# One RWKV-6 block on one core: norm mixes from tiles that ScalarE scales in PSUM

## The chip, the cores and the metric

The kernel runs on one core of a Trainium2 chip. The metric is the device time of one execution in microseconds (us), as the median of several runs. The engines are named as in the profile: PE (TensorE), DVE (VectorE), ACT (ScalarE), POOL (GpSimd) and SP (SyncE, which here only issues DMAs). All arithmetic is in float32.

## The reference, cut to what matters

The input `x` holds 32 sequences of 128 tokens with 512 features. Each sequence goes through one RWKV-6 block. Both of its halves begin with a layer norm and a "token shift": the row before minus the row itself, where the row before the first token comes from a given state.

```python
def _ln(x, w, b): ...          # (x - mean) * rsqrt(var + EPS) * w + b
def _token_shift(xn, prev_row):
    first = (prev_row - xn[:, 0])[:, None]
    rest = xn[:, :-1] - xn[:, 1:]
    return jnp.concatenate([first, rest], axis=1)

xn = _ln(x, ln1_w, ln1_b)                       # first norm
sx = _token_shift(xn, state[:, i1])
xxx = jnp.tanh((xn + sx * maa_x) @ maa_w1)...   # then @ maa_w2, five parts
x5 = xn[:, :, None] + sx[:, :, None] * (maa_stack + xxx)
...                                             # w, r, k, v, g from x5; the recurrence; group norm
x = x + att * g @ Wo.T
xn2 = _ln(x, ln2_w, ln2_b)                      # second norm
sx2 = _token_shift(xn2, state[:, i0])
xk = xn2 + sx2 * ffn_maa_k
xr = xn2 + sx2 * ffn_maa_r
rr = jax.nn.sigmoid(xr @ ffn_Wr.T)
kk = jnp.square(jax.nn.relu(xk @ ffn_Wk.T))
x = x + rr * (kk @ ffn_Wv.T)
```

The row difference of the first norm, `sx`, is used six times (once for `maa_x`, five times for `x5`); that of the second norm, `sx2`, only in the two mixes `xk` and `xr`.

## The kernel before, in words

The 32 sequences are worked in eight groups of four. A group's tile of tokens is 512 columns wide (4 sequences x 128 tokens) and the 512 features lie in four chunks `e` of 128 partitions. For each group these streams exist, each a Python generator:

- `front_mix`: loads `x`, does the first norm, the row difference `sx`, the mix `xin`, and then the five mixed inputs `x5` (lines L433 on PE, L438 and L440 on DVE).
- `front_proj` and `front_gate`: the projections w, k, v, r and g (L389 on PE), evicted by ACT (L499) and sent by DMA into a layout with one head per partition.
- `prep`: the states and products that the recurrence needs (L562, L583, L593, L601 and others on DVE).
- the recurrence, for eight groups one after the other, in units: ACT fills a PSUM tile `sc` (L638) and a column (L649), POOL multiplies and adds (L663, L667), DVE scans (L685) and multiplies (L687, into `rm`), and PE sums over eight transposes (L720, into `acc`).
- `back`: the group norm, the output projection (L788 transposes, L797 scaling on ACT, L799 on DVE, L808 matmuls, L817 adding to `x`), the second norm, and the feed-forward part (the `fk` matmuls at L389, `fr` at L861, `fv` at L877). For the last group it runs twice, on two halves of two sequences each, with half-size tiles (`last1`, `last2`).

Both norms go through `layernorm_T`. It computes the statistics, normalises the rows on ACT (L342), transposes each chunk on PE into a PSUM tile `ps` (L358), and ACT evicts that tile, with the norm's weight and bias, into the SBUF tile `xnT` (L352). `xnT` has one column more than the tokens, for the row before the first token, so the row before and the row itself are the same tile read with an offset of 0 and 1. When all four chunks are there, one DVE instruction makes the row difference (L366; L370 for a half):

```python
nc.vector.tensor_tensor(
    sx.t.rearrange("p e (b t) -> p (e b) t", t=L), xnT[:, :, 0:L], xnT[:, :, 1 : L + 1], ALU.subtract)
```

Then `mix` makes each mix with four DVE instructions (L383), `sx * v + xnT`, all three tiles in SBUF: once after the first norm (`xin`), twice after the second (`xk` ahead of the `fk` matmuls, `xr` after the first of them has been issued).

The order of instructions on each engine is not written by hand. Every generator yields operations with their engine, an estimated duration, what they read and write and which buffer they need, and a list scheduler (`Plan`) takes, again and again, the operation that could start first by its own estimates. Among those that could start within `EPSILON` of the first it prefers the one whose stream is most due, by the table `DUE`. The result is one fixed order per engine; at run time an engine waits where its next instruction's inputs or buffer aren't there. `PE_GAP` is what the planner adds to every operation of PE. Buffers have tags: `ps` is a ring of four PSUM tiles that all matmul results, the transposes and some DVE products share; `sc` has two PSUM tiles, `acc` one; `mx` three SBUF tiles, `xnT` and `sx` one each.

Of the kernel before, what the change touches and what calls it, by code (L numbers as in the profile page):

```python
# [8 lines left out]
F32 = mybir.dt.float32  # L9
I32 = mybir.dt.int32  # L10
AF = mybir.ActivationFunctionType
ALU = mybir.AluOpType
# [23 lines left out]
PE, DVE, ACT, POOL, SP = range(5)  # L36
PASS = 0.43
GAP = 0.034
PE_GAP = 0.09

WINDOW, KEEP, WAKE = 3.41, 0.4, 0.7
LANDING = 2.0
HOP = (0.2, 0.05, 0.05, 0.04, 0.08)
EPSILON = 0.0988


DUE = {"rec": (-0.042, 0.99), "mix": (-1.355, -0.244), "proj": (-1.038, 0.138), "gate": (0.041, 0.061), "prep": (0.365, 1.041), "back": (0.971, 2.191), "last1": (0.877, 1.621), "last2": (1.287, 1.307)}


class Buf:  # L50
# [129 lines left out]
def rwkv6_block(ctx: ExitStack, tc: tile.TileContext, x, prev, s0, vecs, u, maa_w1, maa_w2,  # L180
# [40 lines left out]

    vec = const.tile([P, NV, NE], F32, name="vec")
    pv = const.tile([P, 2, NE, B], F32, name="pv")
    u_sb = const.tile([P, S], F32, name="u_sb")
    w1_sb = const.tile([P, NE, 5 * XM], F32, name="w1_sb")
    w2p = const.tile([P, 4, E], F32, name="w2p")
# [74 lines left out]
    def part(us, bs):  # L301

        return us if len(bs) == GB else us * len(bs) / GB + 0.03

    def layernorm_T(g, src, sums, vw, vb, which, need=None, bs=range(GB)):

        b0, nb_ = bs[0], len(bs)
        bsl, cols = slice(b0, b0 + nb_), slice(b0 * L, (b0 + nb_) * L)  # L310
        if sums is None:
            xh = src
            stats, mv = yield Op(DVE, 0.88, r=[(src, b0)], w=[(0, b0), (1, b0)], alloc=["stats", "mv"])
            for b in bs:
                if b != b0:
                    yield Op(DVE, 0.88, r=[(src, b)], w=[(stats, b), (mv, b)])
                nc.vector.bn_stats(stats[:, b, :], src[:, b, :])
                nc.vector.bn_aggr(mv[:, b, :], stats[:, b, :])
            stats.open = False
            mean, var, scale = mv[:, bsl, 0], mv[:, bsl, 1], 1.0  # L320
        else:
            mv = sums
            yield Op(DVE, 0.16, r=[(mv, b) for b in bs], w=[(mv, "m")])
            mean, var, scale = mv[:, bsl, 0], mv[:, bsl, 1], 1.0 / E
            nc.vector.tensor_scalar(mean, mean, -1.0 / E, None, ALU.mult)
            xh = None
            for b in bs:
                if xh is None:
                    (xh,) = yield Op(ACT, 0.83, r=[(src, b), (mv, "m")], w=[(0, b), (mv, ("v", b))], alloc=["ev"])
                else:  # L330
                    yield Op(ACT, 0.83, r=[(src, b), (mv, "m")], w=[(xh, b), (mv, ("v", b))])
# [12 lines left out]
        rstd.open = nb.open = False  # L344
        (xnT,) = yield Op(ACT, 0.25, w=[(0, "p")], alloc=["xnT"], need=need)
        nc.scalar.copy(xnT[:, :, 0].rearrange("p (e b) -> p e b", b=GB)[:, :, bsl],
                       pv[:, 1 - which, :, g * GB + b0 : g * GB + b0 + nb_])
        late = []

        def evict(e, pt):  # L350
            yield Op(ACT, part(0.78, bs), r=[(pt, None)], w=[(xnT, e)], end=[pt])
            nc.scalar.activation(xnT[:, e * GB + b0 : e * GB + b0 + nb_, 1 : L + 1], bt(pt[:, cols]), AF.Identity,  # L352
                                 bias=col(vb, e), scale=col(vw, e))

        for e in range(NE):
            (pt,) = yield Op(PE, 0.11 * nb_, r=[(xh, None)], w=[(0, None)], alloc=["ps"])
            for b in bs:
                nc.tensor.transpose(pt[:, b * L : (b + 1) * L], xh[:, b, e * P : (e + 1) * P], ident)  # L358
# [6 lines left out]
        if nb_ == GB:  # L365
            nc.vector.tensor_tensor(  # L366
                sx.t.rearrange("p e (b t) -> p (e b) t", t=L), xnT[:, :, 0:L], xnT[:, :, 1 : L + 1], ALU.subtract)
        else:
            xv = xnT.t.rearrange("p (e b) t -> p e b t", b=GB)[:, :, bsl]
            nc.vector.tensor_tensor(sx.t.rearrange("p e (b t) -> p e b t", t=L)[:, :, bsl], xv[:, :, :, 0:L],  # L370
                                    xv[:, :, :, 1 : L + 1], ALU.subtract)
        return xnT, sx

    def mix(xnT, sx, v, bs=range(GB)):

        o = None
        b0, b1 = bs[0], bs[-1] + 1
        for e in range(NE):
            if o is None:
                (o,) = yield Op(DVE, part(0.74, bs), r=[(xnT, None), (sx, None)], w=[(0, e)], alloc=["mx"], port=True)  # L380
            else:
                yield Op(DVE, part(0.74, bs), r=[(xnT, None), (sx, None)], w=[(o, e)], port=True)
            nc.vector.scalar_tensor_tensor(bt(o[:, e, b0 * L : b1 * L]), bt(sx[:, e, b0 * L : b1 * L]), col(v, e),  # L383
                                           xnT[:, e * GB + b0 : e * GB + b1, 1 : L + 1], ALU.mult, ALU.add)
        return o

    def matmuls(p, w, xin, e, cols=slice(0, N)):
        for c in range(NE):
# [12 lines left out]
    def front_mix(g, d):  # L401
# [2 lines left out]
        if g == 0:  # L404
            constants()
        need = (lambda: "ln2" in data[g - 3]) if g > 2 else None
        xnT, sx = yield from layernorm_T(g, xt, None, V_LN1W, V_LN1B, 0, need)
        xin = yield from mix(xnT, sx, V_MAAX)
# [334 lines left out]
    def back(g, d, bs=range(GB), W=None):  # L743
# [81 lines left out]
        xnT, sx = yield from layernorm_T(g, x1, sums, V_LN2W, V_LN2B, 1, need, bs)  # L825
        fkt = yield from get("fk", fk)
        xk = yield from mix(xnT, sx, V_FK, bs)
        frt = yield from get("fr", fr)
        kk, late = None, []
        for e in range(NE + 1):  # L830
            if e < NE:
                (p,) = yield Op(PE, 2 * len(bs) * PASS, r=[(xk, None), (fkt, None)], w=[(0, None)], alloc=["ps"])
                matmuls(p[:, cols], fkt, xk, e, cols)
                late.append(p)
                if e == 0:
                    xr = yield from mix(xnT, sx, V_FR, bs)
                    xnT.open = sx.open = False
# [100 lines left out]
```

## Time and profile before

| | us |
|---|---|
| median of three runs (lowest, highest) | 1603.89 (1602.61, 1604.11) |
| the profiled execution, its own time | 1601.06 |
| its span, first to last instruction | 1599.3 |
| L366 and L370, row differences | 49.1 and 2.4 |
| L383, mixes, 88 full and 16 half tiles | 101.3 |

In a line of engine sums, the first number is the busy time of the engine in us, then its share of the span, then its instructions. The slices cut the span into 40 parts of 40 us; each digit is the busy share in tenths, 9 for 90% or more. In a group's line stand the line of the code, engine, operation, output and inputs by name, their sizes, the count, the busy time in us and the mean of one in ns, and after the second bar the idle time of that engine just before these instructions with what ended it. In a line of waits stand who waited for whom, the sum in us, the number of waits and the longest. In the table by stage, each engine has its busy us in the stretch and its instructions.

### The profile page before, as it was taken

How to read it: one execution, taken by the hardware profiler on the slowest of the kernel's cores; microseconds unless marked ns; L12 is line 12 of the kernel's file. 1: busy time of each engine (PE TensorE's matmuls, PEld its weight loads, DVE VectorE, ACT ScalarE, POOL GpSimd, SP SyncE). 2: the span in 40 equal slices, each digit the busy share in tenths (PEclk: the TensorE clock that was granted, in tenths of full speed). 3: DMA queues.
4: the chain of work that ended last, by engine and by line, in shares of the span. 5: the costliest groups of instructions: out<-in, count | busy, mean ns of one | idle time of the engine just before them, and what ended most of it. 6: DMA issues, size and time to landing. Idle time of an engine off the chain costs nothing.

```text
span 1599.3 us, 16204 instructions
## 1 busy us (share of the span) xinstructions
PE 1477.0 (92%) x5216; PEld 768.9 (48%) x5216; DVE 1374.0 (86%) x1687; ACT 565.9 (35%) x1109; POOL 940.9 (59%) x545
## 2 busy tenths in 40 slices
PE   5997898999999999999999999999999999977978
PEld 2343454454554554545454555445444454444544
DVE  6448999999989999989989999899988899688752
ACT  3222332443334333353333433343323433234242
POOL 4026792886637775578455765478645784477700
PEclk9998999999999999999999999999999999988989
DMA  6220332323224231422323332242313222230230
GB/s 214 60 75 27 93 93 79 120 94 99 66 94 140 66 119 50 138 86 75 103 73 129 119 99 70 96 135 66 119 56 106 92 91 101 85 132 2 75 108 27
DMA packets 126790, 146.85 MB, mean 92 GB/s; under 512 B 8081, under 2 KB 76305, under 8 KB 125681
## 3 DMA queue, kind: packets, MB, share of 16 engines
q1 hardware_dynamic: 91888, 129.03, 24.6%
q10 hardware_dynamic: 34816, 16.79, 3.6%
q8 instruction: 41, 0.67, 0.2%
q14 instruction: 45, 0.36, 0.1%
HBM read 94.41 MB, written 17.83 MB: 70 GB/s over the span
## 4 chain that ended last, share of the span: by engine, by line
PE 50%; DVE 36%; issue 6%; POOL 3%; DMA 2%; ACT 2%; SPq 0%; DVEq 0%; ACTq 0%; POOLq 0%
PE ps L389 14%; DVE sc L685 9%; PE ps L877 7%; PE acc L720 7%; PE ps L808 7%; PE ps L861 7%; DVE rm L687 6%; DVE ps L438 4%; DVE mx L440 3%; DVE mx L383 3%; PE ps L433 2%; DVE sx L366 2%; POOL am L663 2%; PE ps L467 1%; POOL a L667 1%
## 5 line engine op out<-in xcount | busy, mean ns | idle before, releaser
L663 POOL TENSOR_TENSOR am<-v,k 128x1024 f32<-128x1024 f32 x256 | 630.7, 2464 | 185.5 <-DVE k L562 65.4
L389 PE MATMUL ps<-mx,wt 128*128 128x512 f32 (+1 forms) x1312 | 581.2, 590 | 20.3 <-DVE blk L522 6.6
L667 POOL TENSOR_TENSOR a<-am 128x504 f32<-128x504 f32 x256 | 279.6, 1092 | 359.6 <-DVE sc L685 314.8
L389 PEld LDWEIGHTS ps<-mx,wt 128*128 128x128 f32 x1312 | 244.4, 192 | 298.5 <-issue 260.2
L687 DVE TENSOR_TENSOR rm<-sc,r 128x1024 f32<-128x1024 f32 x256 | 312.9, 1222 | 43.7 <-PE acc L720 28.0
L720 PEld LDWEIGHTS acc<-by_head,rm 128*128 128x128 f32 x2176 | 250.1, 143 | 170.5 <-DVE rm L687 81.0
L720 PE MATMUL acc<-by_head,rm 128*128 128x128 f32 x2176 | 285.8, 279 | 48.7 <-DVE rm L687 42.6
L685 DVE TENSOR_TENSOR_SCAN sc<-sc,a 128x512 f32<-128x512 f32 x256 | 312.7, 1222 | 9.0 <-POOL a L667 4.9
L638 ACT COPY sc<-w 128x512 f32<-128x512 f32 x256 | 151.4, 592 | 269.6 <-DVE rm L687 206.1
L433 PE MATMUL ps<-tha,w2p 128*128 128x512 f32 x256 | 129.6, 618 | 8.6 <-DVE mx L440 5.7
L438 DVE SCALAR_TENSOR_TENSOR ps<-ps,vec,sx 128x512 f32<-128x512 f32 x160 | 119.8, 749 | 19.9 <-PE ps L433 19.9
L649 ACT COPY a<-st 128x8 f32<-128x8 f32 x256 | 51.8, 203 | 217.5 <-DVE sc L685 206.3
L808 PE MATMUL ps<-wt,mx 128*128 128x512 f32 x256 | 118.9, 611 | 2.4 <-DVE mx L799 1.0
L861 PE MATMUL ps<-wt,mx 128*128 128x512 f32 x256 | 115.2, 592 | 0.0
L440 DVE TENSOR_TENSOR mx<-ps,xnT 128x512 f32<-128x512 f32 x160 | 110.4, 690 | 4.8
L383 DVE SCALAR_TENSOR_TENSOR mx<-sx,vec,xnT 128x512 f32<-128x512 f32 (+1 forms) x104 | 101.3, 1032 | 0.5
L877 PE MATMUL ps<-wt,ev 128*128 128x512 f32 x224 | 100.8, 592 | 0.0
L499 ACT COPY blk<-ps 128x512 f32<-128x512 f32 x96 | 56.0, 583 | 80.3 <-PE ps L389 62.8
L808 PEld LDWEIGHTS ps<-wt,mx 128*128 128x128 f32 x256 | 47.8, 195 | 61.7 <-issue 50.7
L861 PEld LDWEIGHTS ps<-wt,mx 128*128 128x128 f32 x256 | 47.9, 190 | 56.9 <-issue 55.0
L433 PEld LDWEIGHTS ps<-tha,w2p 128*128 128x128 f32 x256 | 44.1, 195 | 49.4 <-issue 23.7
L366 DVE TENSOR_TENSOR sx<-xnT 128x2048 f32<-128x2048 f32 x15 | 49.1, 3272 | 17.8 <-ACT xnT L352 17.8
(97 smaller groups left out, 1173.8 us busy)
## 6 DMA issues: line engine op xcount, KB each, us to landing
x<-in_x SPq DMA_DIRECT2D x15, 1024.0 KB
wt<-in_wk SPq DMA_DIRECT2D x8, 1024.0 KB
wt<-in_wr SPq DMA_DIRECT2D x8, 1024.0 KB
wt<-in_wg SPq DMA_DIRECT2D x8, 1024.0 KB
dgate<-blk SPq DMA_DIRECT2D x32, 256.0 KB
wt<-in_wo SPq DMA_DIRECT2D x8, 1024.0 KB
wt<-in_fk SPq DMA_DIRECT2D x8, 1024.0 KB
wt<-in_fr SPq DMA_DIRECT2D x8, 1024.0 KB
```

The costliest lines, as they stand in the source:

```text
L389: nc.tensor.matmul(p, lhsT=w[:, c, e * P : (e + 1) * P], rhs=xin[:, c, cols], start=(c == 0), stop=(c == NE - 1))
L433: nc.tensor.matmul(pp.t, lhsT=w2[:, e * P : (e + 1) * P], rhs=lo, start=True, stop=True)
L438: nc.vector.scalar_tensor_tensor(pp.t, pp.t, col(V_MAA + m, f), sx[:, f, :], ALU.add, ALU.mult)
L440: nc.vector.tensor_tensor(bt(x5[:, f, :]), bt(pp.t), xnT[:, f * GB : (f + 1) * GB, 1 : L + 1], ALU.add)
L663: nc.gpsimd.tensor_tensor(am.t, v[:, ds, :], k[:, q : q + 1, :].to_broadcast([P, DH, L]), ALU.mult)
L667: nc.gpsimd.tensor_tensor(a[:, :, 1:T2], am2[:, :, 0 : T2 - 1, 0], am2[:, :, 0 : T2 - 1, 1], ALU.add)
L685: nc.vector.tensor_tensor_scan(scf, scf, a.t.rearrange("p d n -> p (d n)"), 0.0, ALU.mult, ALU.add)
L687: nc.vector.tensor_tensor(pair(rm.t), sc.t.unsqueeze(3).to_broadcast([P, DH, T2, 2]), r2[:, q : q + 1, :, :].to_broadcast([P, DH, T2, 2]), ...
L720: nc.tensor.matmul(acc[:, i, :], lhsT=rm[:, i, :], rhs=by_head, is_transpose=True, start=(q == 0 and i % 4 == 0), stop=(q == S), skip_grou ...
L808: nc.tensor.matmul(p.t, lhsT=att[:, c, b * L : (b + 1) * L], rhs=wot[:, c, :], start=(c == 0), stop=(c == NE - 1))
L861: nc.tensor.matmul(p.t, lhsT=xr[:, c, b * L : (b + 1) * L], rhs=frt[:, c, :], start=(c == 0), stop=(c == NE - 1))
L877: nc.tensor.matmul(p2.t, lhsT=kv[:, c, b * L : (b + 1) * L], rhs=fvt[:, c, :], start=(c == 0), stop=(c == NE - 1))
```

## The change

Four things are changed, and the planner's constants with them.

1. **First norm.** After ACT has evicted a transposed chunk into `xnT`, it scales the same chunk once more, in place in PSUM, with the same weight and bias. DVE then makes that chunk's row difference (row before from `xnT` in SBUF, row itself from PSUM) and at once its mix `xin`. The row difference is therefore four instructions in place of one.
2. **Second norm.** The row difference is not made. A mix is written as `before * m + (1 - m) * itself`. For `xk`, ACT scales the chunk in PSUM in place with the constants `(1 - m) * weight` and `(1 - m) * bias`, and one DVE instruction per chunk adds `m` times the row before. For `xr` (a new function `receptance`), ACT writes `(1 - m)` times the chunk of `xnT` into a new `ps` tile, and DVE adds in the same way.
3. **Constants.** Four small POOL instructions at the start make `ffn`, the products with `1 - m`.
4. **Order.** `back` may begin only when the group's gates are there too; `PE_GAP` goes from 0.09 to 0.04, `EPSILON` from 0.0988 to 0.02, and every entry of `DUE` has another value. The instructions of the other streams stay the same in kind and number, but their order on each engine differs in many places.

```diff
-PE_GAP = 0.09
+PE_GAP = 0.04
...
-EPSILON = 0.0988
+EPSILON = 0.02
...
-DUE = {"rec": (-0.042, 0.99), "mix": (-1.355, -0.244), "proj": (-1.038, 0.138), "gate": (0.041, 0.061), "prep": (0.365, 1.041), "back": (0.971, 2.191), "last1": (0.877, 1.621), "last2": (1.287, 1.307)}
+DUE = {"rec": (0.073, 0.928), "mix": (-1.183, -0.487), "proj": (-1.108, 0.725), "gate": (-0.487, 0.788), "prep": (11.173, 11.194), "back": (1.114, 2.212), "last1": (-8.358, -8.236), "last2": (1.752, 11.136)}
...
         nc.sync.dma_start(out=vec, in_=vecs)
+        nc.gpsimd.tensor_scalar(ffn[:, 0, :], vec[:, V_FK, :], -1.0, 1.0, ALU.mult, ALU.add)
+        nc.gpsimd.tensor_scalar(ffn[:, 2, :], vec[:, V_FR, :], -1.0, 1.0, ALU.mult, ALU.add)
+        nc.gpsimd.tensor_tensor(ffn[:, 1, :], ffn[:, 0, :], vec[:, V_LN2B, :], ALU.mult)
+        nc.gpsimd.tensor_tensor(ffn[:, 0, :], ffn[:, 0, :], vec[:, V_LN2W, :], ALU.mult)
...
         def evict(e, pt):
-            yield Op(ACT, part(0.78, bs), r=[(pt, None)], w=[(xnT, e)], end=[pt])
+            yield Op(ACT, part(0.78, bs), r=[(pt, None)], w=[(xnT, e)])
             nc.scalar.activation(xnT[:, e * GB + b0 : e * GB + b0 + nb_, 1 : L + 1], bt(pt[:, cols]), AF.Identity,
                                  bias=col(vb, e), scale=col(vw, e))
+            yield from use(xnT, e, pt, tiles)
...
-        (sx,) = yield Op(DVE, part(2.3, bs), r=[(xnT, None)], w=[(0, None)], alloc=["sx"], port=True)
...
-            nc.vector.scalar_tensor_tensor(bt(o[:, e, b0 * L : b1 * L]), bt(sx[:, e, b0 * L : b1 * L]), col(v, e),
-                                           xnT[:, e * GB + b0 : e * GB + b1, 1 : L + 1], ALU.mult, ALU.add)
...
+        def use(xnT, e, pt, tiles):
+
+            yield Op(ACT, 0.75, w=[(pt, None)])
+            nc.scalar.activation(pt.t, pt.t, AF.Identity, bias=col(V_LN1B, e), scale=col(V_LN1W, e))
+            sx, xin = tiles
+            yield Op(DVE, 0.69, r=[(xnT, e), (xnT, "p"), (pt, None)], w=[(sx, e)])
+            nc.vector.tensor_tensor(bt(sx[:, e, :]), row(xnT, e, 0), bt(pt.t), ALU.subtract)
+            yield Op(DVE, 0.75, r=[(pt, None), (sx, e)], w=[(xin, e)], end=[pt])
+            nc.vector.scalar_tensor_tensor(xin[:, e, :], sx[:, e, :], col(V_MAAX, e), pt.t, ALU.mult, ALU.add)
...
-        yield Op(DVE, 0.0, need=lambda: d.get("rec"))
+        yield Op(DVE, 0.0, need=lambda: "rec" in d and ("gate", NE - 1) in d)
...
+        def use(xnT, e, pt, tiles):
+
+            yield Op(ACT, part(0.75, bs), w=[(pt, None)])
+            nc.scalar.activation(pt[:, cols], pt[:, cols], AF.Identity, bias=ffn[:, 1, e : e + 1], scale=ffn[:, 0, e : e + 1])
+            (xk,) = tiles
+            yield Op(DVE, part(0.75, bs), r=[(xnT, e), (xnT, "p"), (pt, None)], w=[(xk, e)], end=[pt])
+            nc.vector.scalar_tensor_tensor(bt(xk[:, e, cols]), row(xnT, e, 0, bs), col(V_FK, e), bt(pt[:, cols]),
+                                           ALU.mult, ALU.add)
+
+        def receptance(xnT):
+            xr = None
+            for e in range(NE):
+                if xr is None:
+                    pr, xr = yield Op(ACT, part(0.75, bs), r=[(xnT, e)], w=[(0, None)], alloc=["ps", "mx"])
+                else:
+                    (pr,) = yield Op(ACT, part(0.75, bs), r=[(xnT, e)], w=[(0, None)], alloc=["ps"])
+                nc.scalar.activation(bt(pr[:, cols]), row(xnT, e, 1, bs), AF.Copy, scale=ffn[:, 2, e : e + 1])
+                yield Op(DVE, part(0.75, bs), r=[(xnT, e), (pr, None)], w=[(xr, e)], end=[pr])
+                nc.vector.scalar_tensor_tensor(bt(xr[:, e, cols]), row(xnT, e, 0, bs), col(V_FR, e), bt(pr[:, cols]),
+                                               ALU.mult, ALU.add)
+            return xr
...
-            xr = yield from mix(xnT, sx, V_FR, bs)
+            xr = yield from receptance(xnT)
```

More of the change, by code (lines that the diff above doesn't have):

```diff
@@ L223, in rwkv6_block @@
     pv = const.tile([P, 2, NE, B], F32, name="pv")
+    ffn = const.tile([P, 3, NE], F32, name="ffn")
     u_sb = const.tile([P, S], F32, name="u_sb")
@@ L303, in part, with layernorm_T @@
         return us if len(bs) == GB else us * len(bs) / GB + 0.03
-    def layernorm_T(g, src, sums, vw, vb, which, need=None, bs=range(GB)):
+    def layernorm_T(g, src, sums, vw, vb, which, use, take, need=None, bs=range(GB)):
         b0, nb_ = bs[0], len(bs)
@@ L350, in evict @@
         def evict(e, pt):
-            yield Op(ACT, part(0.78, bs), r=[(pt, None)], w=[(xnT, e)], end=[pt])
+            yield Op(ACT, part(0.78, bs), r=[(pt, None)], w=[(xnT, e)])
             nc.scalar.activation(xnT[:, e * GB + b0 : e * GB + b0 + nb_, 1 : L + 1], bt(pt[:, cols]), AF.Identity,
                                  bias=col(vb, e), scale=col(vw, e))
+            yield from use(xnT, e, pt, tiles)
         for e in range(NE):
-            (pt,) = yield Op(PE, 0.11 * nb_, r=[(xh, None)], w=[(0, None)], alloc=["ps"])
+            if e == 0:
+                pt, *tiles = yield Op(PE, 0.11 * nb_, r=[(xh, None)], w=[(0, None)], alloc=["ps", *take])
+            else:
+                (pt,) = yield Op(PE, 0.11 * nb_, r=[(xh, None)], w=[(0, None)], alloc=["ps"])
             for b in bs:
@@ L363, in layernorm_T, with row @@
         yield from evict(*late.pop(0))
-        (sx,) = yield Op(DVE, part(2.3, bs), r=[(xnT, None)], w=[(0, None)], alloc=["sx"], port=True)
[L365 to L383, printed above, removed]
-                                           xnT[:, e * GB + b0 : e * GB + b1, 1 : L + 1], ALU.mult, ALU.add)
-        return o
+        return (xnT, *tiles)
+    def row(xnT, e, shift, bs=range(GB)):
+        return xnT[:, e * GB + bs[0] : e * GB + bs[-1] + 1, shift : shift + L]
     def matmuls(p, w, xin, e, cols=slice(0, N)):
@@ L406, in front_mix @@
         need = (lambda: "ln2" in data[g - 3]) if g > 2 else None
-        xnT, sx = yield from layernorm_T(g, xt, None, V_LN1W, V_LN1B, 0, need)
-        xin = yield from mix(xnT, sx, V_MAAX)
+        def use(xnT, e, pt, tiles):
[6 more added lines that the diff above has]
+            nc.vector.scalar_tensor_tensor(xin[:, e, :], sx[:, e, :], col(V_MAAX, e), pt.t, ALU.mult, ALU.add)
+        xnT, sx, xin = yield from layernorm_T(g, xt, None, V_LN1W, V_LN1B, 0, use, ("sx", "mx"), need)
         d["xin"] = True
@@ L824, in back @@
         need = (lambda: "mixed" in data[g + 2]) if g + 2 < NG else None
-        xnT, sx = yield from layernorm_T(g, x1, sums, V_LN2W, V_LN2B, 1, need, bs)
+        def use(xnT, e, pt, tiles):
[10 more added lines that the diff above has]
+                    pr, xr = yield Op(ACT, part(0.75, bs), r=[(xnT, e)], w=[(0, None)], alloc=["ps", "mx"])
+                else:
+                    (pr,) = yield Op(ACT, part(0.75, bs), r=[(xnT, e)], w=[(0, None)], alloc=["ps"])
[4 more added lines that the diff above has]
+            return xr
+        xnT, xk = yield from layernorm_T(g, x1, sums, V_LN2W, V_LN2B, 1, use, ("mx",), need, bs)
         fkt = yield from get("fk", fk)
-        xk = yield from mix(xnT, sx, V_FK, bs)
         frt = yield from get("fr", fr)
@@ L835, in back @@
                 if e == 0:
-                    xr = yield from mix(xnT, sx, V_FR, bs)
-                    xnT.open = sx.open = False
+                    xr = yield from receptance(xnT)
+                    xnT.open = False
                     d["ln2"] = True
```

## Prediction

> **What bounds the kernel now.** I read the busy line and the slices first, then the chain, the costliest groups, a table of busy time by stage, and who ended TensorE's waits.
>
> ```profile
> PE 1477.0 (92%) x5216; PEld 768.9 (48%) x5216; DVE 1374.0 (86%) x1687; ACT 565.9 (35%) x1109; POOL 940.9 (59%) x545
> PE   5997898999999999999999999999999999977978
> DVE  6448999999989999989989999899988899688752
> PE 50%; DVE 36%; issue 6%; POOL 3%; DMA 2%; ACT 2%; SPq 0%; DVEq 0%; ACTq 0%; POOLq 0%
> ```
>
> PE and DVE are both full in the middle, and the chain that ended last changes between them; ScalarE (ACT) has room. The share averages over stages, so I asked for busy time by stage (columns: PE, PEld, DVE, ACT, POOL, each with its instructions; then clock and DMA):
>
> ```profile
> 150.00:200.00 50.00, 42.81 (x151) 21.75 (x151) 48.58 (x53) 16.16 (x33) 36.93 (x22) 0.89 0.24 74
> 200.00:400.00 200.00, 185.17 (x686) 96.99 (x684) 192.12 (x237) 72.39 (x146) 139.99 (x79) 0.98 0.31 97
> ...
> 800.00:1000.00 200.00, 195.93 (x708) 102.01 (x707) 186.91 (x222) 75.64 (x147) 128.79 (x71) 1.00 0.30 98
> ```
>
> From 150 to 400 us DVE bounds: 240.7 of 250 us busy, PE 228.0. From 400 to 1400 us PE bounds: the five stretches sum to 970.5 of 1000 us, DVE to 920.4. So a cheaper DVE can win there only what PE still loses to DVE. Who ended PE's waits between 400 and 1200 us:
>
> ```profile
> PE acc L720 <- DVE rm L687: 9.9, 12, 1.9
> PE ps L389 <- ACT ev L851: 3.1, 4, 1.0
> PE ps L433 <- DVE mx L440: 2.9, 4, 1.7
> PE ps L358 <- ACT xnT L352: 1.7, 4, 0.4
> ```
>
> With the small rows DVE ended 15.8 us of PE's waits there, and 5.5 us more in 1200 to 1400: 21.3 us out of 29.5 us of PE idle time.
>
> The rows that the change deletes, and those that price what it adds:
>
> ```profile
> L366 DVE TENSOR_TENSOR sx<-xnT 128x2048 f32<-128x2048 f32 x15 | 49.1, 3272 | 17.8 <-ACT xnT L352 17.8
> L383 DVE SCALAR_TENSOR_TENSOR mx<-sx,vec,xnT 128x512 f32<-128x512 f32 x88 | 94.8, 1133 | 0.5
> L440 DVE TENSOR_TENSOR mx<-ps,xnT 128x512 f32<-128x512 f32 x160 | 110.4, 690 | 4.8
> L438 DVE SCALAR_TENSOR_TENSOR ps<-ps,vec,sx 128x512 f32<-128x512 f32 x160 | 119.8, 749 | 19.9 <-PE ps L433 19.9
> L797 ACT ACTIVATE ps<-ps,vec 128x512 f32<-128x512 f32 x28 | 20.9, 751 | 10.1 <-PE ps L788 9.9
> L472 ACT ACTIVATE blk<-ps,vec 128x512 f32<-128x512 f32 x32 | 21.9, 685 | 27.9 <-DMA w<-blk 16.8 <-PE ps L467 8.8 <-PE acc L720 2.3
> ```
>
> The reader is to see that a mix from two SBUF tiles (L383) takes 1133 ns where the same operation with one operand in PSUM (L438) takes 749.
>
> [...] at 770.86 us, while POOL stood idle (768.7 to 776.3), four L383 took 2.74 us (685 ns each); at 20.59 us, beside POOL's L292, four took 4.30 us (1075 ns each). [...]
>
> **The change part by part.**
>
> DVE removed: L366 49.1, its half form L370 2.4, L383 101.3 (94.8 and 6.5 for halves): 152.8 us. DVE added: first norm, eight groups of four subtractions at 0.690 (L440's form) and four mixes at 0.750 (L438's): 46.1. Second norm: 28 full and 8 half tiles, each mixed twice: 56 x 0.750 + 16 x 0.482 [...] = 49.7. Sum 95.8; DVE does 57 us less. Per steady group: the first norm 3.3 + 4 x 1.08 = 7.6 becomes 5.8, the second 3.3 + 8 x 1.08 = 11.9 becomes 6.0, so -7.7 us. Bounds of the unseen mixes: 0.69 (L868, no pointer scalar) to 0.80; 4 us in all either way.
>
> ACT added: scaling in place, 60 x 0.751 and 8 x 0.532 (L797's two forms), 49.3; the receptance copies from SBUF to PSUM with one pointer, 28 x 0.685 and 8 x 0.47, 23.0: 72 us. ACT goes from 566 to 638 us, 40% of the span. It lies beside other work, but ACT's queue also carries the recurrence's fills (L638, L649), which now stand behind evictions that wait for a transpose. They had slack: ACT waited 206 us for L687 to give an sc tile back. POOL gets four 128x4 instructions at the start; its 7.2 us of idle time before L337 hides them. The DMAs stay as many (484 from SP, 256 from ACT), and POOL's other instructions too.
>
> By stage, against the profiled execution's own 1601.1 us (span 1599.3; the median of the runs is 2.8 us above it):
>
> - **0 to 150 us: 0.** The first mix would feed PE (L412) about 4 us sooner, but DVE then still has eight statistics to do (L317, L318) from x tiles that land at 25.9 us, and the order after keeps them ahead of the first L438. That wait for DMA is late next and hides the gain.
> - **150 to 400: -5.7.** DVE bounds. The first norm at 241 us (2.27 + 4.42) becomes 5.8, the second's row difference and first mix at 391 (3.11 + 4.71) becomes 3.0.
> - **400 to 1400: -14.** DVE loses 42 us of 920, but PE can only give back the 21.3 us it waited for DVE. The row difference and its mixes stand as blocks of 7 to 9 us in DVE's queue, with recurrence units behind them; in the order after they are single instructions between units. I take two thirds; the last third stays because L687 in turn waits for PE to free its rm tile (21.9 us in this stage). Next late is PE itself.
> - **1400 to 1530: -3.** The norm at 1450 us (2.29 + 7.35) becomes 6.0; recurrence units there also run into POOL (78 of 100 us busy).
> - **1530 to the end: +2.** The order after puts the second half's first two transposes ahead of the first half's last four. They wait for the y that DVE finished at 1536.5, where PE before had begun at 1530.2. Seven ACT scalings (about 0.49 us apart) then end near 1540 and the first matmuls of L808's kind with them; before, that block ended at 1541.3 at a lowered clock. Between 0 and +5.
> - **PSUM tiles: +5.** The ps ring has four buffers. The order shows 36 more ps tiles (636 to 672), and 68 norm tiles held through one more ACT and one or two DVE instructions: 104 tiles, over 2 us longer each. What PE pays for it no row shows. Below: 0, since the tiles of the first mix and L440 already pass with 5.7 + 4.4 us of PE waits; above: 0.4 us a tile (the longest wait of L358 for a norm tile), 42 us. I take 0.05.
>
> Sum -15.7: 1585.4 against 1601.1, so 1588 as a median of runs. The re-tuned planner constants have no row; I take 0 with 10 us either way, since the order keeps the same 854 PE rows and the same sequence of stages.
>
> **The rivals.** 0.2% of 1604 is 3.2 us, about what a measurement of this kernel can tell from no change.
>
> - **DVE and PE give back more** (0.20). In the chain L383 and L366 hold 4.8% of the span, 77 of the 153 us that go. If the chain shortens in that proportion, 57 x 77/153 = 29 us go, and the smaller blocks win a few more: 1570 to 1575. Against it: behind these links PE had only 29.5 us idle in 1000.
> - **PE bounds it all** (0.14). The freed DVE time shows as idle time; only 150 to 400 us gains, less the ps tiles: 1598 to 1606. For it: PE's 97%.
> - **Slower: the ps ring** (0.20). PE and DVE queues run in a fixed order. A transpose, or a matmul of fk, waits for a ps buffer that is held for a scaling or a mix queued behind recurrence units, and all of PE's queue stands behind it. With 20.7 us of gain it decides from 0.20 us a tile on; at 0.4 it costs 42 and the kernel takes 1625, at 0.3 it takes 1614. For it: four buffers, and receptance tiles that ACT and DVE fill and empty while fk's matmuls want the same ring. Against it: the longest such wait now is 0.4 us.
>
> **How the numbers follow.** The forecast (0.46) has its own range of 1578 to 1600. All its cases and the first rival are faster, and a little of the second: 0.46 + 0.20 + 0.05. No change, 0.07, is the most of the rest of the second; slower is the third rival and what is left, 0.22. The range reaches down past the first rival with the tuning's 10 us, to 1562, and up to 0.3 us a tile, 1613.
>
> **What would show it.** Right: rows L366 and L383 gone; new DVE rows near 690 and 750 ns with DVE's sum near 1317 us; ACT near 638; PE's sum unchanged near 1477 and its share 93%; PE's waits for L687 shorter between 400 and 1400 us; POOL's multiply L663 below its 2464 ns. Wrong: PE waits on ps tiles released by the new ACT or DVE lines beyond 10 us in sum, new mixes over 0.9 us, or DVE idle time that grew by the whole 57 us while the span stayed.

## The result, and the profile after

The kernel after takes 1586.05 us (median of four runs, 1584.49 to 1586.98), the kernel before beside it 1603.25 (four runs, 1602.19 to 1604.11). The ratio is 0.9892, with a 95% interval of 0.9875 to 0.9909: 17 us faster. The forecast was 1588. One execution of the last tail run below took 2228.6 us at a granted clock of 0.65, where its others have 0.97 to 0.98; it is in none of the ratios. The profiled execution of the kernel after took 1586.62 us, its span 1584.8.

The engine sums, PE's and DVE's slices and the chain's shares by engine, from the page of the kernel after:

```profile
PE 1470.4 (93%) x5216; PEld 771.2 (49%) x5216; DVE 1321.9 (83%) x1702; ACT 632.7 (40%) x1213; POOL 919.0 (58%) x549
PE   5898799899989999999999999999999999978778
DVE  5539899999989999989979999888988999697642
PE 68%; DVE 17%; POOL 8%; issue 3%; ACT 1%; DMA 1%; SPq 0%; DVEq 0%; POOLq 0%
```

DVE does 52.1 us less and ACT 66.9 us more. PE's sum is nearly the same (6.6 us less), so most of the time went where PE stood idle. DVE's part of the chain falls from 36% to 17%, PE's rises from 50% to 68%. The added instructions, from the groups with their shapes kept apart (after the second bar: idle time of the engine ahead of them, and who ended it):

```profile
L408 DVE SCALAR_TENSOR_TENSOR mx<-sx,vec,ps 128x512 f32<-128x512 f32 x32 | 23.9, 748 | 1.1
L406 DVE TENSOR_TENSOR sx<-xnT,ps 128x512 f32<-128x512 f32 x32 | 21.8, 680 | 21.7 <-ACT ps L403 21.6
L833 DVE SCALAR_TENSOR_TENSOR mx<-xnT,vec,ps 128x512 f32<-128x512 f32 x28 | 20.6, 735 | 5.3 <-ACT ps L830 5.3
L845 DVE SCALAR_TENSOR_TENSOR mx<-xnT,vec,ps 128x512 f32<-128x512 f32 x28 | 20.3, 734 | 0.0
L830 ACT ACTIVATE ps<-ps,ffn 128x512 f32<-128x512 f32 x28 | 21.0, 750 | 0.9
L843 ACT ACTIVATE ps<-xnT,ffn 128x512 f32<-128x512 f32 x28 | 19.1, 689 | 16.5 <-DVE mx L845 10.2 <-issue 3.3 <-DMA v<-blk 2.7
```

These stand at the durations that were forecast: 680 to 748 ns, where the deleted mix took 1133 in the mean. That mean mixes two kinds. Of the 88 full-sized L383 of the kernel before, 60 overlapped no POOL instruction and took 736 to 752 ns, as long as a new one; the other 28 did, and took 1970 in the mean. The new lines show no such difference (L406 680 and L408 748 ns with POOL beside them or not). So a new mix is cheaper mostly because it isn't stretched beside POOL's work. Half-sized, the new rows took 479 and 480 ns on DVE (L833, L845) and 537 and 465 on ACT (L830, L843). The forecast had 0.482 us for the first, an estimate of its author's, and 0.532 and 0.47 for the others; the deleted L383 of that size had taken 480 ns.

PE's waits between 400 and 1200 us:

```profile
PE ps L790 <- DVE y L779: 4.1, 1, 4.1
PE ps L382 <- DVE mx L845: 3.3, 5, 1.3
PE ps L435 <- DVE mx L801: 2.8, 4, 0.7
PE ps L884 <- DVE mx L408: 2.7, 2, 1.5
PE ps L382 <- DVE mx L442: 2.4, 1, 2.4
PE acc L722 <- DVE rm L689: 2.0, 2, 1.2
```

The wait for `rm` fell from 9.9 us to 2.0. The new lines L845 and L408 hold 6.0 us.

**Where the time went, stage by stage.** The same stretches of the clock show this, in the table of busy time of the kernel after:

```profile
150.00:200.00 50.00, 37.15 (x127) 18.04 (x125) 43.95 (x52) 13.55 (x29) 34.81 (x20) 0.86 0.27 85
200.00:400.00 200.00, 192.08 (x720) 102.48 (x720) 188.70 (x236) 84.81 (x166) 137.21 (x82) 0.99 0.33 104
...
800.00:1000.00 200.00, 195.93 (x699) 102.20 (x698) 179.68 (x227) 84.93 (x160) 123.12 (x73) 1.00 0.30 93
```

From 800 to 1000 us PE is busy for the same 195.93 us in both kernels. But a stretch of the clock holds other work in the two kernels, and busy time is not work. I therefore cut both traces at landmarks of the work, the start of the last ACT copy of `acc` into `y` of each group's recurrence, and counted PE's matmuls in each piece at their back-to-back spacing (0.429 us for 512 columns, 0.216 for 256, 0.109 for 128, from dense runs such as L884's eight at 1545.18 us, after which the next instruction starts at 1548.61; the medians from the start of one matmul to the next of the same size, with 128 rows, are 429, 216 and 109 ns in both traces). What a piece lasts beyond that is time that PE lost, idle or with its matmuls further apart:

| piece, ending with | before: ends at, lost | after: ends at, lost | difference of lost |
|---|---|---|---|
| first group's recurrence | 262.6, 62.5 | 264.9, 61.5 | -1.0 |
| seventh group's ("the middle") | 1378.8, 74.7 | 1348.7, 59.0 | -15.7 |
| eighth group's ("the last group") | 1521.5, 37.9 | 1496.8, 33.0 | -4.9 |
| the end ("the tail") | 1599.3, 19.3 | 1584.8, 26.5 | +7.2 |

Both kernels have the same 5216 matmuls, so the differences sum to that between the two spans, -14.5 us, but for rounding. The -1.0 of the first piece is less than what two executions of the kernel after differ by there (61.5 and 59.4). The middle, the last group and the tail are three separate results, and the tail lost.

The middle can be cut once more. Each of its six groups has two copies of `acc`, and in the kernel before all row differences of the middle and 65 of its 68 mixes stand between a group's first copy and its second. The lost time of the six groups, with two of the experiments below:

| the middle's lost time | up to the first copy | from the first to the second |
|---|---|---|
| kernel before | 45.8 | 28.9 |
| kernel after | 46.3 | 12.8 |
| a cheaper mix in the order of before | 45.8 | 17.0 |
| second-norm mixes issued twice, order of after | 48.1 | 52.8 |

The whole gain lies where the mixes stood. Up to the first copy, single groups moved by -6.3 to +6.8 us with the new order, and the sum by only 0.5.

The listed waits show less than that. In the middle, those that DVE ended sum to 33.7 us before and 32.6 after: the wait for `rm` fell from 13.2 to 2.0, but others came in its place, 7.1 us of them for the new lines. Those that ACT ended fell from 6.4 to 0. That is 7.5 us together; the rest of the 15.7 is in no listed wait and was not traced further.

### The profile page after: what moved, and what is told of

The parts are those of the page before. It is cut to its first block, busy times and chain, and to the rows that moved or that the text cites. A ratio compares the mean times of both kernels' runs of the same rounds, so it can differ in the third digit from the quotient of the medians.

```text
span 1584.8 us, 16299 instructions
## 1 busy us (share of the span) xinstructions
PE 1470.4 (93%) x5216; PEld 771.2 (49%) x5216; DVE 1321.9 (83%) x1702; ACT 632.7 (40%) x1213; POOL 919.0 (58%) x549
## 4 chain that ended last, share of the span: by engine, by line
PE 68%; DVE 17%; POOL 8%; issue 3%; ACT 1%; DMA 1%; SPq 0%; DVEq 0%; POOLq 0%
PE ps L382 26%; PE acc L722 10%; PE ps L435 7%; PE ps L884 7%; PE ps L900 6%; PE ps L810 6%; POOL am L665 5%; DVE sc L687 3%; POOL a L669 3%; DVE rm L689 2%; DVE ps L440 2%; PE ps L469 2%; PE ps L461 1%; DVE mx L442 1%; PE ps L417 1%
## 5 line engine op out<-in xcount | busy, mean ns | idle before, releaser
L665 POOL TENSOR_TENSOR am<-v,k 128x1024 f32<-128x1024 f32 x256 | 615.5, 2404 | 211.9 <-DVE k L564 111.2
L382 PE MATMUL ps<-mx,wt 128*128 128x512 f32 (+1 forms) x1312 | 576.3, 587 | 13.4 <-DVE mx L845 5.1
L669 POOL TENSOR_TENSOR a<-am 128x504 f32<-128x504 f32 x256 | 274.9, 1074 | 305.7 <-DVE sc L687 279.0
L382 PEld LDWEIGHTS ps<-mx,wt 128*128 128x128 f32 x1312 | 244.3, 191 | 288.5 <-issue 265.7
L687 DVE TENSOR_TENSOR_SCAN sc<-sc,a 128x512 f32<-128x512 f32 x256 | 312.9, 1222 | 15.9 <-POOL a L669 13.1
L722 PE MATMUL acc<-by_head,rm 128*128 128x128 f32 x2176 | 281.4, 276 | 19.7 <-DVE rm L689 12.8
L435 PE MATMUL ps<-tha,w2p 128*128 128x512 f32 x256 | 137.2, 634 | 20.7 <-DVE mx L442 5.9
L440 DVE SCALAR_TENSOR_TENSOR ps<-ps,vec,sx 128x512 f32<-128x512 f32 x160 | 119.8, 749 | 39.3 <-PE ps L435 38.9
L884 PE MATMUL ps<-wt,mx 128*128 128x512 f32 x256 | 115.4, 593 | 4.2 <-DVE mx L408 2.7
L884 PEld LDWEIGHTS ps<-wt,mx 128*128 128x128 f32 x256 | 47.4, 190 | 60.4 <-issue 59.1
L435 PEld LDWEIGHTS ps<-tha,w2p 128*128 128x128 f32 x256 | 43.1, 198 | 61.4 <-issue 21.3
L343 POOL TENSOR_TENSOR rstd<-rstd,mhalf 128x4 f32<-128x4 f32 (+1 forms) x17 | 16.7, 981 | 93.0 <-DVE rstd L341 92.6
L889 DVE SCALAR_TENSOR_TENSOR ps<-th,ps 128x512 f32<-128x512 f32 x32 | 22.1, 689 | 50.6 <-PE ps L900 47.2
```

Source lines behind the costliest of these rows:

```text
L382: nc.tensor.matmul(p, lhsT=w[:, c, e * P : (e + 1) * P], rhs=xin[:, c, cols], start=(c == 0), stop=(c == NE - 1))
L435: nc.tensor.matmul(pp.t, lhsT=w2[:, e * P : (e + 1) * P], rhs=lo, start=True, stop=True)
L440: nc.vector.scalar_tensor_tensor(pp.t, pp.t, col(V_MAA + m, f), sx[:, f, :], ALU.add, ALU.mult)
L665: nc.gpsimd.tensor_tensor(am.t, v[:, ds, :], k[:, q : q + 1, :].to_broadcast([P, DH, L]), ALU.mult)
L669: nc.gpsimd.tensor_tensor(a[:, :, 1:T2], am2[:, :, 0 : T2 - 1, 0], am2[:, :, 0 : T2 - 1, 1], ALU.add)
L687: nc.vector.tensor_tensor_scan(scf, scf, a.t.rearrange("p d n -> p (d n)"), 0.0, ALU.mult, ALU.add)
```

## The experiments

Each kernel ran beside runs of the kernel before. Differences to the kernel after are of medians. "Lost" is PE's time as in the table above.

### Constants alone

The mixes of before with the planner constants and the start condition of after. The entries `rec` and `last1` keep their old values, since the planner finds no order otherwise; so this is not quite the order table of after.

```diff
-PE_GAP = 0.09
+PE_GAP = 0.04
-EPSILON = 0.0988
+EPSILON = 0.02
...
+DUE = {'rec': (-0.042, 0.99), 'mix': (-1.183, -0.487), 'proj': (-1.108, 0.725), 'gate': (-0.487, 0.788), 'prep': (11.173, 11.194), 'back': (1.114, 2.212), 'last1': (0.877, 1.621), 'last2': (1.752, 11.136)}
...
-        yield Op(DVE, 0.0, need=lambda: d.get("rec"))
+        yield Op(DVE, 0.0, need=lambda: "rec" in d and ("gate", NE - 1) in d)
```

> The kernel before, its norms and mixes untouched, with the new PE_GAP and EPSILON, the new start condition of back, and the new DUE except for rec and last1, which keep their old values because the planner finds no order otherwise. If DVE's relief makes the gain (theory A), the constants alone give about nothing: 1596 to 1610 us. If the order of instructions makes it (theory B), most of the 17 us is here: 1585 to 1592 us.

Measured: 1705.65 us, ratio 1.065 (1.0634 to 1.0665). Both theories missed by about 100 us.

### Mixes alone

The mixes of after with the constants and the start condition of before (the same diff backwards, with `DUE`).

> The changed norms and mixes with the planner's constants, DUE and the start condition of back as they were before. Theory A (the mixes): 1584 to 1593 us. Theory B (the constants): 1597 to 1608 us. Should each alone give only a part, the two add up: about 1595 us in each.

Measured: 1698.46 us, ratio 1.0605 (1.0585 to 1.0624); missed just as far, though DVE's sum is low (1319.8 us). PE's waits, first of this kernel, then of the constants alone:

```profile
PE acc L722 <- DVE rm L689: 50.8, 39, 5.7
PE ps L790 <- DVE y L779: 42.9, 6, 9.5
```

```profile
PE acc L720 <- DVE rm L687: 77.8, 49, 6.3
```

In the kernels before and after these waits for `rm` sum to 42.6 and 12.8 us. Neither half of the change works with the constants made for the other. So no effect of the constants alone could be measured that adds to that of the mixes, and "the change without re-tuning" is no kernel that either profile describes.

### Second-norm mixes issued twice

The kernel after in its order, every L833 and L845 issued twice.

```diff
+            nc.vector.scalar_tensor_tensor(bt(xk[:, e, cols]), row(xnT, e, 0, bs), col(V_FK, e), bt(pt[:, cols]),
+                                           ALU.mult, ALU.add)
...
+                nc.vector.scalar_tensor_tensor(bt(xr[:, e, cols]), row(xnT, e, 0, bs), col(V_FR, e), bt(pr[:, cols]),
+                                               ALU.mult, ALU.add)
```

> The changed kernel with each mix of the second norm issued twice on DVE (72 more instructions, 56 x 0.735 + 16 x 0.48 = 49 us; the result is the same), the planner told nothing. If DVE's time is what the span is made of in the middle (theory A as the forecast sized it, two thirds of what DVE loses comes back as time), +20 to +35 us: 1606 to 1621 us. If PE bounds the middle and DVE has idle time to give (theory C), +3 to +12 us: 1589 to 1598 us.

Measured: 1633.47 us, ratio 1.0196 (1.0179 to 1.0213), 47.4 us above the kernel after for 50.6 us more of DVE. Above both expectations. The lost time in the middle rose by 41.9 us (59.0 to 100.9), 40.0 of them between the two copies of a group, where nearly all of the added instructions stand; the last group's rose by 4.2 and the tail's by 2.5. PE's waits for the whole span:

```profile
PE acc L722 <- DVE rm L689: 17.9, 19, 2.4
PE ps L382 <- DVE mx L849: 15.9, 5, 4.5
```

L849 is L845 of the kernel after, where this wait was 5.1 us. It makes `xr`, which the matmuls of L382 don't read; what they can wait for here is a `ps` tile that L849 gives back. So 10.8 us of PE's added waiting came by way of the ring of `ps` tiles, which the added instruction holds longer.

### First-norm difference and mix issued twice

```diff
+            nc.vector.tensor_tensor(bt(sx[:, e, :]), row(xnT, e, 0), bt(pt.t), ALU.subtract)
...
+            nc.vector.scalar_tensor_tensor(xin[:, e, :], sx[:, e, :], col(V_MAAX, e), pt.t, ALU.mult, ALU.add)
```

> The changed kernel with the first norm's row differences and mixes (L406, L408) issued twice, the result the same: 64 more DVE instructions, 32 x 0.680 + 32 x 0.748 = 46 us, about what the doubled mixes of the second norm added (they cost 47 us of time). If DVE's time is what counts wherever it stands (theory A), +35 to +50 us: 1621 to 1636 us. If it was the late xk and the held ps tiles of the second norm (theory C), half or less: under 1610 us.

Measured: 1618.83 us, ratio 1.0095 (1.008 to 1.011), 32.8 us above the kernel after; DVE's sum rose by 42.6 us (1364.5). Just under the range of the first theory and well over the other. Here too the ring has a part: PE's waits for the doubled mix (L410, L408 in the kernel after) went from 3.4 to 13.1 us, those for `rm` from 12.8 to 21.1. With the longer-held tiles counted in, an added microsecond of DVE costs 0.77 us here and 0.94 above: DVE is on the path in the kernel after too, though its share of the span is 83% and PE's 93%.

### A cheaper mix in the order of before

L383 of the kernel before leaves out the addition of the normalised row; the order stays.

```diff
-            nc.vector.scalar_tensor_tensor(bt(o[:, e, b0 * L : b1 * L]), bt(sx[:, e, b0 * L : b1 * L]), col(v, e),
-                                           xnT[:, e * GB + b0 : e * GB + b1, 1 : L + 1], ALU.mult, ALU.add)
+            nc.vector.tensor_scalar(bt(o[:, e, b0 * L : b1 * L]), bt(sx[:, e, b0 * L : b1 * L]), col(v, e), None, ALU.mult)
```

> The kernel before, with each of its 104 mixes replaced by a product of the row difference and the column (the addition of the normalised row is left out), one SBUF tensor input in place of two; the order of every queue stays that of before. DVE loses about 60 us, what the change takes from it, with no ACT instruction, no PSUM tile and no new order. If DVE's time makes the span (theory A), 1565 to 1582 us. If PE bounds the middle (theory C), 1588 to 1600 us.

Measured: 1587.82 us, ratio 0.9904 (0.9889 to 0.9919), 15.0 us under the kernel before. The groups of this kernel, where the row difference is the one that before has at 3272 ns:

```profile
L383 DVE TENSOR_SCALAR mx<-sx,vec 128x512 f32<-128x512 f32 x88 | 71.5, 871 | 0.5
L366 DVE TENSOR_TENSOR sx<-xnT 128x2048 f32<-128x2048 f32 x15 | 50.7, 3383 | 17.9 <-ACT xnT L352 17.9
```

The edit took only 24.0 us off DVE (1374.0 to 1350.0), less than the expectation counted on, since the 28 mixes that overlap POOL stayed stretched, at 1710 ns in the mean (last section); 0.63 us came back for each. In the middle the lost time fell from 74.7 to 63.0 us, in an order and with ACT instructions that nothing else had touched, and it fell only from the first copy to the second, where the cheaper mixes stand; the wait for `rm` fell from 13.2 to 6.3 us. Relief of DVE alone thus gives 11.7 of the 15.7 us by which the middle of the kernel after gained, and in the same places.

### ScalarE's evictions issued twice

The kernel after, L358 and L843 twice: ACT gains 72.5 us, and 104 tiles of `ps` are held longer.

```diff
+            nc.scalar.activation(xnT[:, e * GB + b0 : e * GB + b0 + nb_, 1 : L + 1], bt(pt[:, cols]), AF.Identity,
+                                 bias=col(vb, e), scale=col(vw, e))
...
+                nc.scalar.activation(bt(pr[:, cols]), row(xnT, e, 1, bs), AF.Copy, scale=ffn[:, 2, e : e + 1])
```

> The changed kernel with every eviction of a transposed chunk (L358) and every receptance copy (L843) issued twice on ACT, the result the same and the planner told nothing: 104 more ACT instructions, about 72 us, as much again as the change added, and 104 ps tiles held 0.7 us longer each. The forecast's terms (ACT beside other work, 0.05 us of PE per held tile) give +3 to +10 us: 1588 to 1596 us. If the fixed queues let every late eviction through to PE (the slower rival, from 0.2 us a tile), over +20 us: above 1606 us.

Measured: 1602.15 us, ratio 0.9995 (0.9986 to 1.0003), 16.1 us above the kernel after: more than the forecast's terms, less than the slower rival. By pieces the lost time changed by -1.0, +5.5, +4.0 and +6.6 us. The middle holds 68 of the added instructions (44 of L358, 24 of L843), 0.08 us each; the last two pieces hold 24, 16 of them half-sized, and took 10.6 us, 0.44 us each. A mean of 0.15 us a tile hides two very different prices.

### No scalings

The kernel after without L403 and L830.

```diff
-            nc.scalar.activation(pt.t, pt.t, AF.Identity, bias=col(V_LN1B, e), scale=col(V_LN1W, e))
...
-            nc.scalar.activation(pt[:, cols], pt[:, cols], AF.Identity, bias=ffn[:, 1, e : e + 1], scale=ffn[:, 0, e : e + 1])
```

> The kernel after in the same order, without the 68 in-place scalings on ScalarE (L403 and L830, 24.0 + 25.3 = 49.3 us in its profile). Left out of the computation: weight and bias of both norms in the row that the mixes take from PSUM. Theory A, the longer-held ps tiles and ScalarE's longer queue cost what the doubling of the other 104 ScalarE instructions showed (16.1 us for 72.5 us, 0.22 us for each us): 11 us less than the kernel after, 1572 to 1579. Theory B, the forecast's term of 0.05 us a tile: 68 tiles give 3.4 us, 1581 to 1585. Theory C, the scalings lie wholly beside other work and only more than they cost: within 1 us of the kernel after, 1585 to 1588.

Measured: 1579.68 us (1579.18 to 1579.83), ratio 0.9855 (0.9842 to 0.9869), 6.1 us under the kernel after on the same chip (1585.77): between the ranges of A and B. By pieces the lost time changed by -1.4, -1.2, -2.0 and -2.1 us; the first of these is within the spread of that piece. The middle had 44 scalings, 0.03 us each; the last two pieces had 12, 0.35 us each. Together with the run above, one more ACT instruction of about 0.7 us on a `ps` tile costs 0.03 to 0.08 us in the middle.

### Two other orders for the tail

First, the second half's transposes wait until the first half's projection is issued:

```diff
+        if half and b0:
+            yield Op(PE, 0.0, need=lambda: "att" in d)
...
+                if b == bs[-1]:
+                    d["att"] = True
```

> The changed kernel, with the transposes of the last group's second half held back until the first half's output projection has been issued. From L736's last copy to the end the changed kernel takes 88.0 us, the kernel before 77.8. If that order makes the difference (theory A), 6 to 9 us come back: 1577 to 1580 us. If the tail is longer because the new norm's own instructions are (ACT twice per chunk, theory C), less than 2 us: 1584 to 1587 us.

Measured: 1585.0 us, ratio 0.9896 (0.9881 to 0.9911), no difference to the kernel after, as theory C had it. The second half's group norm still stood ahead of the first half's gated tiles in DVE's queue, and PE waited 3.7 us for those instead. Second, that group norm is held back too:

```diff
+        if half and b0:
+            yield Op(DVE, 0.0, need=lambda: "att" in d)
...
+        d["att"] = True
```

> The changed kernel, with the last group's second half held back one step earlier than in the tail experiment before: its group norm on DVE starts only when the first half's gated tiles are made, so that they no longer stand behind it in DVE's queue. PE waited 3.7 us for them there, and 7.1 us for the first half's y, which stays. If DVE's order was the tail's loss, 5 to 8 us less than the changed kernel: 1578 to 1581 us. If the second half then comes as much later, 1583 to 1586 us.

Measured: 1583.99 us, ratio 0.988 (0.9863 to 0.9896). That is the second of the two ranges. The tail's lost time fell from 26.5 to 23.7 us. Because 2 us is little, this version ran once more beside the kernel after:

> The kernel after, unchanged, on the same chip as the other two of this call, as the base to which they are compared: 1585 to 1588, by every theory.

> The kernel after with the second half's group norm on VectorE held back until the first half's gated tiles are made, a second time, with more rounds and beside the kernel after on the same chip. If the 2 us seen before are real, 1583 to 1585 and under the kernel after by 1 to 3 us; if they were the difference between chips, within 0.5 us of the kernel after.

Measured: ratios 0.9905 (0.9889 to 0.9921) for the kernel after, whose median was 1585.77 us, and 0.9889 (0.9873 to 0.9904) for the tail order, with a median of 1583.81 us. The difference is 0.0016 here, and 0.0012 between the runs made at different times, about 2 to 2.5 us, both times the same way; the intervals overlap, so it isn't separated. It has the lowest ratio of the versions that compute the whole reference, if by little.

## Why the prediction was right, step by step

The total was right, and so were the prices and the cause that it rests on, DVE's relief. Not all of its terms were, and some of the agreement is luck.

- **DVE's work.** Forecast -57 us, measured -52.1. The deleted lines held 152.8 us, the added ones hold 94.0. Of that difference 34 us is what the 28 mixes beside POOL took beyond 742 ns each, and 15 us what 14 row differences beside POOL took beyond the 2291 ns of the one that had no POOL instruction beside it. That the new rows would take 690 and 750 ns, as L440 and L438 did, is as forecast. (Its 685 ns for L383 without POOL is the time of four divided by four; each lasts 746 to 751 and overlaps the next a little.) What is missing is in a row that the change doesn't touch: L595 (L593 before), a product of two SBUF tiles, went from 819 to 1068 ns in 32 instructions, 8.0 us. In both kernels 17 of them overlapped no POOL instruction and took 671 to 701 ns. The other 15 took 965 ns in the mean before and 1497 after: they make up the whole 8.0 us. In the new order POOL is at work in 20.2 us of the time of these 15, where it was in 10.4.
- **0 to 150 us: 0.** Right for the reason given: DVE's wait for `x`, which ends near 26 us, grew from 1.0 to 3.5 us, and the first L438 (L440 after) starts at 34.3 us, where it was 33.7. The order then moved work within this stretch. By 150 us PE was 6.0 us of matmul work ahead, and from 150 to 200 us it gave that back (PE 37.15 us busy where it had been 42.81, with DVE at 43.95 instead of 48.58).
- **150 to 400: -5.7, and 400 to 1400: -14.** Of the -5.7, the first norm's part (6.7 to 5.8 us, -0.9) lies ahead of the first landmark and -4.8 behind it. With -14, and 0.05 us for each of the middle's 68 tiles (+3.4), the middle had -15.4 to come; it got -15.7. Where the mixes stood, the term is borne out: the first group of the middle (to 462.1 us before, 457.9 after) had about -5 to come there, an estimate from these terms, and gave -3.6; the other five had about -10 and gave -12.5. The rest is luck: up to the first copy, the first group won 6.3 us and the other five lost 6.8, which the forecast had at nothing. Of the 6.3, 6.0 are one wait of L389 for L522 that is gone after. It stays in the order of before when the mixes are cheaper, so as far as the runs show, the order took it. The reason given, "PE can only give back the 21.3 us it waited for DVE", fits by half: the waits for `rm` went, but waits for other DVE lines came, so that those which DVE ended fell by just 1.1 us in the middle. In the run with the cheaper mix, where the order stays, they fell by 7.5 us (33.7 to 26.2), as the reason would have it.
- **The last group: -3.** With its eight tiles' 0.4 us, -2.6; measured -4.9.
- **The tail: +2.** This term was mis-sized most: +2.8 us with 0.8 for the 16 half tiles, measured +7.2. The forecast worked out when the first matmul of the output projection would start and stopped there. (The lowered clock that it names is 0.71 from 1530 to 1541.3 us before; over the whole tail the granted clock is 0.90 in both kernels.) PE's waits in the tail, before and then after:

```profile
PE ps L788 <- DVE y L777: 8.7, 1, 8.7
PE ps L808 <- DVE mx L799: 1.0, 1, 1.0
```

```profile
PE ps L790 <- DVE y L779: 11.3, 2, 7.1
PE ps L382 <- DVE mx L833: 1.8, 4, 0.7
PE ps L382 <- DVE mx L845: 1.6, 1, 1.6
PE ps L790 <- DVE mx L801: 0.7, 1, 0.7
```

The waits for `y` grew by 2.6 us; that the second half's transposes would wait was foreseen. The 3.4 us ahead of L382 were not. The 1.8 for L833 come from ACT. Its timeline in the kernel after (start, duration, instruction):

```profile
1532.33 0.56 ACT L358 ACTIVATE xnT<-ps,vec 128x256 f32<-128x256 f32 x1 [1.17 <-PE ps L368]
1532.93 0.54 ACT L830 ACTIVATE ps<-ps,ffn 128x256 f32<-128x256 f32 x1
1533.39 0.56 ACT L358 ACTIVATE xnT<-ps,vec 128x256 f32<-128x256 f32 x1
1533.98 0.54 ACT L830 ACTIVATE ps<-ps,ffn 128x256 f32<-128x256 f32 x1
```

Eviction and scaling alternate, so a mixed chunk comes about every 1.05 us, and PE's next two matmuls take it in step:

```profile
1534.04 0.70 PE L382 MATMUL ps<-mx,wt 128*128 128x256 f32 x2 [0.73 <-DVE mx L833]
1535.09 0.70 PE L382 MATMUL ps<-mx,wt 128*128 128x256 f32 x2 [0.36 <-DVE mx L833]
1536.14 0.70 PE L382 MATMUL ps<-mx,wt 128*128 128x256 f32 x2 [0.35 <-DVE mx L833]
1537.20 0.70 PE L382 MATMUL ps<-mx,wt 128*128 128x256 f32 x2 [0.35 <-DVE mx L833]
1539.48 5.42 PE L382 MATMUL ps<-mx,wt 128*128 128x256 f32 x24 [1.59 <-DVE mx L845]
```

PE's queue has no other work between these matmuls, so each scaling lies on the path: without the scalings the waits for L833 (L831 there) sum to 0.2 us. The 1.6 us for L845 are another matter, and stay at 1.6 without the scalings (L843 there). The matmuls of L382 don't read L845's `xr`; after the first `fk` result, what they can wait for is a `ps` tile that the receptance holds, whose ACT copies (L843) stand among the other half's statistics in ACT's queue (L338, 0.71 us each at 1536.56 and 1537.66). This is the forecast's third rival, at work in the tail. The named waits explain 5.7 of the 7.2 us.

- **The ps tiles: +5.** Plausible in size, but not measured as it was put. The term was for 104 tiles held over 2 us longer, 36 of them new; the two runs vary only about 0.7 us of that, and give 0.03 and 0.08 us a tile in the middle, 0.35 and 0.44 in the last two pieces, where PE lost 59.5 of 236.1 us (in the middle 59.0 of 1083.8). What the kernel after shows directly is PE's waits for a `ps` tile that a new line gives back: 8.5 us in the whole span (L845 5.1, L408 3.4), 0.08 us for each of the 104. The forecast had named 10 us of them as a sign of being wrong, so it was near.
- **The constants: 0 with 10 either way.** As a term of its own this cannot be shown right or wrong: each half alone is about 100 us slower. The reason given, that the order keeps the same stages, was too weak: single groups moved by up to 6.8 us with it, and they cancel in the middle (+0.5) by luck.

The rivals: the 29 us of the first did not come, since the middle gave 15.7. That PE bounds it all fell with the same 15.7 us. The ring needed 0.20 us a tile to win, and its waits come to 0.08. The sum was right because the middle's was; a tail 4.4 us dearer than forecast was met by a start and a last group that were better by 0.7 (-1.0 against -0.3) and 2.3 us. What stays open is how much of the middle's last 4 us (15.7 against 11.7) is the larger relief and how much the order. It is open too why DVE time costs more when added to the order after (0.77 and 0.94) than it returned when taken from the order before (0.63): the longer-held tiles are part of it, but both orders are fixed, and no run varied the order with the load alone.

## What to carry to other kernels

Cut two traces at the same point of the work, not at the same microsecond, and count what the bounding engine lost in each piece: the sum over two such cuts must give the difference of the spans. Cut once more where the changed instructions stand; here that showed that the whole gain of the middle lies there, and that a forecast can be right in a piece's sum and wrong in its parts. Split a mean duration by what ran beside the instruction before calling it a price: L383's 1133 ns were 742 and 1970. Price an added hop twice, once in the middle and once in the tail: here one cost 0.03 and 0.08 us a tile in the one, 0.35 and 0.44 in the last two pieces. Where a scheduler's constants belong to a change, measure them together: here each half alone took about 1700 us (1705.65 and 1698.46), where the two together take 1586.05, and told of neither.

## What was not expected of the hardware

A tensor-scalar with a single SBUF input of 128x512 took 871 ns in the mean in the kernel with the cheaper mix, more than the 735 to 748 ns of the new mixes that read one tile from SBUF and one from PSUM. The half-sized ones, all in the tail with no POOL instruction beside them, took 348:

```profile
L383 DVE TENSOR_SCALAR mx<-sx,vec 128x256 f32<-128x256 f32 x16 | 4.4, 348 | 0.1
```

The trace settles why. Of the 88 full-sized ones, 60 overlapped no POOL instruction and took 472 to 488 ns; the other 28 took 625 to 2566, in the mean 1710. The deleted mix with two SBUF inputs splits into the same numbers, 60 at 742 ns and 28 at 1970 in the mean. So dropping an operand saved about 260 ns on either kind, and both lose about 1.23 us more in the mean where POOL is at work, with one SBUF input as well as with two. No run stopped POOL, but none of these instructions was long without POOL beside it. Two lines of the kernel before that read one tile from PSUM don't show it: L440 took 690 ns in the mean, both for the 49 that overlapped no POOL instruction and for the 111 that did, and L438 751 ns for 40 and 748 for 120.
